# Tensor-product sums by five column-tiled matmuls per edge tile, with the product's scalar part put together by a constant matrix

## The chip, the cores and the metric

The kernel runs on one core of a Trainium2 chip. The time is the device time in microseconds (us) of one execution; the time before is the median of three runs, 1883.51 us (1879.14 to 1885.42). The engines of the core run side by side, each in the order of its own instructions, and meet at semaphores: TensorE (PE for its matmuls, PEld for its weight loads), VectorE (DVE), ScalarE (ACT), GpSimd (POOL) and SyncE (SP), the last two mostly issuing transfers here.

## What is computed

Four graph layers run one after another on 625 nodes and 20,000 edges sorted by receiver, each on a normalised copy of `x` and each added to `x`. The change lies in the third, a tensor product of node features with edge directions:

```python
s0, s1 = x0[sender], x1[sender]            # 128 scalars, 128 vectors of 3 per edge
y0, y1 = edge_attrs[:, 0:1], edge_attrs[:, 1:4]
p1 = w1 * s0 * y0
p2 = (w2 * s0)[:, :, None] * y1[:, None, :]
p3 = w3[:, :, None] * s1 * y0[:, None, :]
p4 = w4 * einsum('eum,em->eu', s1, y1) / SQRT3     # a sum over the vector's 3 parts
msg0 = segment_sum(concatenate([p1, p4], -1), receiver)
msg1 = segment_sum(concatenate([p2, p3], 1), receiver)
o0, o1 = _lin_irreps(msg0, msg1, W_out0, W_out1)
```

`w1` to `w4` come from a small network on eight radial features of each edge (`mlp` in the kernel). So for each receiver eight rows of 128 numbers are summed: one for p1, three for p2, three for p3, and one for p4, which is itself a sum of three products.

## The kernel before

The edges stand in 160 tiles of 125 (`NT`), four tiles to a group (`G`, 40 groups), eight to a step of the gathers and masks. Because the edges are sorted by receiver, the receivers of a group lie within a window of `W` = 32 nodes, which begins at `base_of(g)`. The third layer is `layer2_near`, and its main loop goes over pairs of tiles (80 of them):

- `rows` (line 230 issues it) gathers the senders' rows of the next eight tiles, by GpSimd's indirect transfers.
- `hots` makes the masks on VectorE: `eq` has a 1 where an edge's receiver is the window's node (line 819), and `ohy` holds four masks, `eq` times each of the edge's four attributes y0, y1x, y1y, y1z (line 826).
- `product` makes for each tile the weights `tpw` by a matmul of 64 rows (line 834), the two tiles of a pair on the two halves of the array, and from it on VectorE `msg` of eight blocks: `m[:, 0, 0:4]` is w1 s0 and the three w3 s1, `m[:, 1, 0:4]` is w2 s0 and the three w4 s1 (in two operations, lines 839 and 841).
- `scatter2`, two pairs behind, multiplies the masks with these blocks and sums over the edges of the tile (line 856). A mask has 32 columns, so the result fills 32 rows of a bank: four such column groups of the array, each with its own 32 output rows, hold different sums (`tile_position`). The accumulator `sum` is of 128 rows by three blocks of 128 columns; a group of four tiles is summed in it.
- `evict` copies it by ScalarE (line 873), and `collect`, another two pairs behind, turns it by TensorE (line 881) and adds it to the window's columns of `mT2` on VectorE (line 884).
- `radial` (lines 786 and 791) runs the small network for later tiles, in between.
- `nodes` does the last part for 125 nodes as soon as their last group is collected: output matmuls from `mT2` (line 912; `order` tells which two of its eight rows belong together), the norm, transposes (line 925), and two tables for the next layer (line 932).

Before, `scatter2` issues eight matmuls per tile, and the scalar part p4 is summed over its three products in the accumulator itself, since the three go to the same place. In row r of the column groups and block c, `add(r, c, q, v)` sums mask q times `v`:

| column group | block 0 | block 1 | block 2 |
|---|---|---|---|
| 0 | p1 | p3 x | p3 y |
| 1 | p3 z | p2 x | |
| 2 | p2 y | p2 z | |
| 3 | p4 (three matmuls) | | |

The instructions of each engine are put in order when the program is built, by a scheduler that follows data and buffers; in this layer no order is held by hand. Buffers: two `sum` banks, two shared by `mlp` and `trs`, four of `tpw`; seven `msg` tiles.

Of the kernel before, what the change touches and what calls it, by code (L numbers as in the profile page):

```python
# [9 lines left out]
F32 = mybir.dt.float32  # L10
# [17 lines left out]
MUL = 128  # L28
# [115 lines left out]
def gnn_body(ctx: ExitStack, tc: tile.TileContext, a: dict, out: bass.AP, consts, near: bool):  # L144

    nc = tc.nc
# [603 lines left out]
    def layer2_near(w2s, w1ab, wm3a, uh, h, tab, loads):  # L750

        W = 32
        NS = NT // (2 * G)
        with tc.tile_pool(name="layer2n", bufs=2) as lp, \
                tc.tile_pool(name="ps2n", bufs=1, space=bass.MemoryType.PSUM) as pp:
            def ps2(name):
                return pp.tile([128, 512], F32, tag="ps", name=name, bufs=2)
# [41 lines left out]
            got, sums, ohs, msgs = {}, {}, {}, {}  # L799

            def base_of(g):
                return min(max(math.ceil(g * G * PACE - SLACK), 0), N - W)
# [41 lines left out]

            def scatter2(s, i):

                g = 2 * s + i // 2
                if i % 2 == 0:
                    sums[g] = pp.tile([128, 3 * MUL], F32, tag="sum", name="sum", bufs=2)
                A = sums[g]  # L850
                for j in (2 * i, 2 * i + 1):
                    m, oh = msgs.pop((s, j)), ohs[s][0]
                    done = set()

                    def add(r, c, q, v):
                        nc.tensor.matmul(A[r * W:(r + 1) * W, c * MUL:c * MUL + v.shape[1]], oh[:, j, q, :], v,  # L856
                                         start=j % G == 0 and r not in done, stop=j % G == G - 1,
                                         skip_group_check=True, tile_position=(0, r * W))
                        done.add(r)

                    add(0, 0, 0, m[:, 0, 0:3, :].rearrange("p k u -> p (k u)"))
                    add(1, 0, 0, m[:, 0, 3, :])
                    add(2, 0, 2, m[:, 1, 0, :])
                    add(3, 0, 1, m[:, 1, 1, :])
                    add(1, 1, 1, m[:, 1, 0, :])
                    add(2, 1, 3, m[:, 1, 0, :])
                    add(3, 0, 2, m[:, 1, 2, :])
                    add(3, 0, 3, m[:, 1, 3, :])

            def evict(g):  # L870
                v = lp.tile([128, 3 * MUL], F32, tag="sv", name="sv")
                for n, c in ((128, 0), (96, 1), (32, 2)):
                    nc.scalar.copy(v[:n, c * MUL:(c + 1) * MUL], sums[g][:n, c * MUL:(c + 1) * MUL])
                sums[g] = v

            def collect(g):
                v = sums.pop(g)
                t = ps2("trs")
                o = 0
                for n, c in ((128, 0), (96, 1), (32, 2)):  # L880
                    nc.tensor.transpose(t[:, o:o + n], v[:n, c * MUL:(c + 1) * MUL], ident[:n, :n])
                    o += n
                b = base_of(g)
                nc.vector.tensor_add(mT[:, :, b:b + W], t[:, :o].rearrange("p (k n) -> p k n", n=W),
                                     mT[:, :, b:b + W])
# [2 lines left out]

            last_of = [max(g for g in range(NG) if base_of(g) < (c + 1) * P) for c in range(NC)]
            so = 1.0 / (math.sqrt(2.0 * MUL) * 10.0)  # L890
            order = ((0, 3), (5, 4), (2, 7), (6, 1))
            h3 = node.tile([P, NC, D], F32, tag="h", name="h3")
            tabs = [dram.tile([N, D], F32, tag=v, name=v) for v in ("xs", "xd")]
            stats = {}
# [50 lines left out]
            for i in range(len(pairs) + LAG + 2):  # L945
                if i < len(pairs):
                    s, j = pairs[i]
                    product(s, j)
                    q, step = divmod(i, 2 * G)
                    if 2 <= 2 * q < NS - 2 and step in (1, 3, 5):  # L950
                        radial(q + 1, step // 2)
                    if s + 1 < NS:
                        if j == 0:
                            rows(s + 1)
                        hots(s + 1, j)
                if 0 <= i - LAG < len(pairs):
                    s, j = pairs[i - LAG]
                    scatter2(s, j)
                    if j % 2:
                        evict(2 * s + j // 2)  # L960
                if 0 <= i - LAG - 2 < len(pairs):
                    s, j = pairs[i - LAG - 2]
                    if j % 2:
                        collect(2 * s + j // 2)
                for c in range(NC - 1):
                    step = i - (2 * last_of[c] + LAG + 3)
                    if 0 <= step < 5:
                        nodes(c, step)
                if i in loads:
                    loads[i]()  # L970
# [462 lines left out]
    with tc.tile_pool(name="wts3", bufs=1) as wts:  # L1433
# [3 lines left out]
        if near:  # L1437
# [18 lines left out]
            def load_own():  # L1456
                keep(nc.scalar.dma_start(wm3a, chunks(a["L3_gnn_W3"][:D, :])))

            h_tabs = layer2_near(w2s, w1ab, wm3a, uh, h2, tab2, {6: load_nodes, 30: load_edges, 50: load_own})
            layer3_near(wts, wm2, (b1, b2, w1c), h_tabs, uh)  # L1460
        else:
# [44 lines left out]
```

## Time and profile before

| what | value |
|---|---|
| median of the runs | 1883.51 us |
| the profiled execution | 1883.0 us |
| its span | 1881.2 us |
| mean granted TensorE clock | 0.983 |
| third layer's sums (line 856), first and last start | 670.2 and 998.5 us |
| busy from 660 to 1000 us: TensorE matmuls / VectorE / ScalarE / GpSimd | 321 / 245 / 71 / 197 of 340 us |
| line 856, recorded passes (two for each matmul) | 2560 |
| line 881, the three turns of each group | 120 |
| line 884, the addition | 40 of 421 ns |

The profile is of one execution. A group of instructions is named by line, engine, operation and tiles (`sum<-msg,ohy` writes `sum` from `msg` and `ohy`), a shape is partitions by columns, and "x32" counts instructions. A matmul of 32-bit numbers is recorded as two passes, each with its own weight load (LDWEIGHTS); a transpose is one. The ends of matmuls are modelled, so the spacing of starts tells more than the lengths. In the chain of work that ended last, each instruction is followed back to what released it; "issue" is time in which an engine waited for nothing that the profile shows. The idle time ahead of an instruction is put down to its releaser.

### The profile page before, as it was taken

The page shows a single profiled execution, that of the slowest core. Times are in us where ns is not written, and L with a number is a line of the kernel's source. Part 1 is how long each engine was busy: PE and PEld are TensorE (multiplying, and loading weights), DVE is VectorE, ACT ScalarE, POOL GpSimd, SP SyncE. Part 2 cuts the span into 40 slices and gives each one's busy share as a digit, 9 for nine tenths or more (in the row PEclk, how much of TensorE's full clock was granted, in tenths as well). Part 3 has the DMA queues.
Part 4 walks back from the last instruction along what each step waited for, and adds up shares of the span by engine and source line. Part 5 has one row for each costly group of instructions (what it writes and reads, how often), then busy time and mean ns, then how long its engine had stood idle before and what let it go on. Part 6 is the DMA issues. An engine that isn't in the chain of part 4 may idle for free.

```text
span 1881.2 us, 25801 instructions
## 1 busy us (share of the span) xinstructions
PE 1772.1 (94%) x10688; PEld 960.7 (51%) x10688; DVE 1074.1 (57%) x1877; ACT 741.3 (39%) x856; POOL 809.9 (43%) x478
## 2 busy tenths in 40 slices
PE   5999999999999999999999989999999999999993
PEld 5999844444444444445455444444454444545441
DVE  8999611001100267768774657786676676666655
ACT  1122211000000312222221766767776777668670
POOL 0000000000000077556543688888887888788200
PEclk9999999999999989999999989999999999999996
DMA  2000103003000176565443589666675666666200
GB/s 70 2 2 2 52 0 140 0 0 93 2 0 0 30 187 162 139 146 161 125 119 98 116 150 172 127 122 119 109 132 114 115 132 116 109 119 125 36 0 13
DMA packets 157223, 162.68 MB, mean 86 GB/s; under 512 B 97546, under 2 KB 104059, under 8 KB 157096
## 3 DMA queue, kind: packets, MB, share of 16 engines
q0 software_dynamic: 131584, 119.48, 32.4%
q1 hardware_dynamic: 20100, 32.69, 5.7%
q10 hardware_dynamic: 5412, 8.77, 1.7%
q8 instruction: 86, 1.41, 0.3%
q14 instruction: 41, 0.34, 0.1%
HBM read 155.11 MB, written 5.12 MB: 85 GB/s over the span
## 4 chain that ended last, share of the span: by engine, by line
PE 83%; DVE 11%; ACT 2%; DMA 2%; issue 1%; POOL 0%; DVEq 0%; SPq 0%; ACTq 0%; POOLq 0%
PE z L1243 29%; PE agg L557 9%; PE hb L544 7%; PE sum L856 7%; PE tpw L834 5%; DVE rh L441 4%; PE z L1224 4%; PE z L1229 4%; DVE ohs L450 2%; PE agg L1267 2%; PE xsd L932 2%; PE mlp L786 2%; PE agg L533 2%; PE l L509 2%; PE nsum L502 1%
## 5 line engine op out<-in xcount | busy, mean ns | idle before, releaser
L1243 PE MATMUL z<-wm,z 128*125 128x512 f32 x1280 | 556.9, 593 | 2.7 <-DVE z L1362 2.7
L1243 PEld LDWEIGHTS z<-wm,z 128*125 128x125 f32 x1280 | 237.5, 188 | 293.5 <-issue 268.8
L230 POOL DMA_INDIRECT g_s<-xs,src_i x160 | 303.4, 1896 | 126.1 <-issue 75.5
L230 POOL DMA_INDIRECT g_s<-xd,dst_i x144 | 300.6, 2087 | 43.9 <-issue 42.0
L798 POOL MEMSET mT<- 128x5000 f32 x1 | 4.3, 4267 | 633.4 <-PE agg L557 633.4
L230 POOL DMA_INDIRECT gup<-up,src_i x160 | 198.1, 1238 | 132.0 <-DVE msg L841 60.6
L455 PE MATMUL q<-rh,ohs 125*128 125x160 bf16 (+1 forms) x2400 | 184.5, 238 | 13.5 <-ACT cnt L467 11.0
L455 PEld LDWEIGHTS <-ohs 125*128 125x128 bf16 x2400 | 180.0, 99 | 17.8 <-issue 15.0
L1245 DVE TENSOR_TENSOR mess<-z,b 125x512 f32<-125x512 f32 x160 | 106.4, 687 | 136.4 <-PE z L1243 136.4
L557 PE MATMUL agg<-hb,adj 125*125 125x512 f32 x400 | 173.6, 592 | 0.0
L547 DVE COPY hb<-hb 125x512 f32<-125x512 f32 x20 | 13.8, 692 | 261.0 <-PE hb L544 261.0
L856 PE MATMUL sum<-msg,ohy 125*32 125x128 f32 (+1 forms) x2560 | 146.0, 303 | 8.5 <-issue 6.9
L841 DVE TENSOR_TENSOR msg<-tpw,gup 125x768 f32<-125x768 f32 x160 | 152.0, 950 | 0.0
L856 PEld LDWEIGHTS sum<-msg,ohy 125*32 125x32 f32 x2560 | 101.2, 109 | 86.7 <-issue 85.7
L1231 DVE TENSOR_SCALAR z<-z,b 128x500 f32<-128x500 f32 (+1 forms) x164 | 108.4, 719 | 59.4 <-PE z L1229 57.5
L544 PE MATMUL hb<-basis,hT 128*125 128x512 f32 x320 | 138.6, 592 | 0.0
L1191 ACT ACTIVATE uz<-uz 128x2000 f32<-128x2000 f32 (+1 forms) x41 | 75.0, 1830 | 153.0 <-DVE uz L1183 153.0
L557 PEld LDWEIGHTS agg<-hb,adj 125*125 125x125 f32 x400 | 74.8, 188 | 94.7 <-issue 94.7
L549 ACT COPY hb<-hb 125x512 f32<-125x512 f32 x20 | 11.7, 586 | 258.3 <-PE hb L544 238.4
L839 DVE TENSOR_TENSOR msg<-tpw,gup 125x256 f32<-125x256 f32 x160 | 67.0, 419 | 62.9 <-PE tpw L834 31.1
L1191 ACT ACTIVATE um<-um 125x2048 f32<-125x2048 f32 x39 | 74.6, 1912 | 71.1 <-DVE um L1183 71.1
L544 PEld LDWEIGHTS hb<-basis,hT 128*125 128x125 f32 x320 | 60.1, 188 | 77.3 <-issue 76.8
(187 smaller groups left out, 2240.5 us busy)
## 6 DMA issues: line engine op xcount, KB each, us to landing
rt<-in_edge_attr SPq DMA_DIRECT2D x76, 125.0 KB
basis<-in_L_gnn_basis SPq DMA_DIRECT2D x8, 1024.0 KB
gup<-up,src_i POOLq DMA_INDIRECT x160
g_s<-xs,src_i POOLq DMA_INDIRECT x160
g_s<-xd,dst_i POOLq DMA_INDIRECT x144
w<-in_L_gnn_W SPq DMA_DIRECT2D x2, 1024.0 KB
loop<-in_L_gnn_loop SPq DMA_DIRECT2D x2, 1024.0 KB
w1ab<-in_L_gnn_W ACTq DMA_DIRECT2D x1, 2048.0 KB
```

What stands on the lines that cost most here:

```text
L230: return nc.gpsimd.indirect_dma_start(out=dst, out_offset=None, in_=table, in_offset=bass.IndirectOffsetOnAxis(ap=idx[:, t:t + 1], axis=0) ...
L441: keep(nc.vector.tensor_mul(rh, eq[:, :, None, :].to_broadcast([P, G, 3 * NQ + 1, W]), parts[:, t0:t0 + G, :, None] .to_broadcast([P, G, 3 ...
L455: nc.tensor.matmul(q[c][:, :n, o:o + W], os_[:, c, :], rh[:, j, q0:q0 + n, :], start=i + j + k == 0, stop=i == 1 and j == G - 1 and k == 2 ...
L544: nc.tensor.matmul(p[:P, :], hT[:, k, s * P:(s + 1) * P], basis[b][:, k, :], start=k == 0, stop=k == KD - 1)
L557: nc.tensor.matmul(acc[c], adj[:, s - 1, l * NB + b, c * P:(c + 1) * P], hb[:, b, :], start=False, stop=s == NC and b == NB - 1)
L834: nc.tensor.matmul(p[:P, :], hid[s // 2][s % 2][rws, i * P:(i + 1) * P], w4[rws].rearrange("p k u -> p (k u)"), start=True, stop=True)
L841: nc.vector.tensor_mul(m[:, :, 1:, :], pv[:, 2:4, None, :].to_broadcast([P, 2, 3, MUL]), g[:, None, 1:, :].to_broadcast([P, 2, 3, MUL]))
L856: nc.tensor.matmul(A[r * W:(r + 1) * W, c * MUL:c * MUL + v.shape[1]], oh[:, j, q, :], v, start=j % G == 0 and r not in done, stop=j % G = ...
L1191: keep(nc.scalar.activation(u, u, AF.Exp))
L1231: keep(nc.vector.tensor_scalar(zv[:, n, f, :], pf[f][:, :ne], b1[:, f:f + 1], None, op0=ALU.add))
L1243: nc.tensor.matmul(p[:P, :], z[:, j // w, f, j % w * P:(j % w + 1) * P], wm2[:, f, :], start=f == 0, stop=f == KD - 1)
L1245: keep(nc.vector.tensor_add(m[:, j, :], p[:P, :], bc["b2"]))
```

## The change

The three products of p4 are no longer added in one place. In the new layout each of the column groups 1 to 3 takes one direction, and one matmul of two blocks sums a p2 and a p4 part with the same mask:

| column group | block 0 | block 1 | block 2 |
|---|---|---|---|
| 0 | p1 | p3 x | p3 y |
| 1 | p2 x | p4, part x | p3 z |
| 2 | p2 y | p4, part y | |
| 3 | p2 z | p4, part z | |

```diff
-                    add(0, 0, 0, m[:, 0, 0:3, :].rearrange("p k u -> p (k u)"))
-                    add(1, 0, 0, m[:, 0, 3, :])
-                    add(2, 0, 2, m[:, 1, 0, :])
-                    add(3, 0, 1, m[:, 1, 1, :])
-                    add(1, 1, 1, m[:, 1, 0, :])
-                    add(2, 1, 3, m[:, 1, 0, :])
-                    add(3, 0, 2, m[:, 1, 2, :])
-                    add(3, 0, 3, m[:, 1, 3, :])
+                    add(0, slice(0, 3), 0, m[:, 0, 0:3, :])
+                    for r in range(1, 4):
+                        add(r, slice(0, 2), r, m[:, 1, 0:r + 1:r, :])
+                    add(1, slice(2, 3), 0, m[:, 0, 3:4, :])
```

So a tile has one matmul of 384 columns, three of 256 and one of 128, where it had one of 384 and seven of 128; the columns in all are the same 1280. The parts of p4 are added when the accumulator is turned: block 1 is not transposed but multiplied by a constant matrix `fold` of 64 columns, the first 32 of which pick column group 0, the last 32 the sum of groups 1 to 3. It is made once, by three small VectorE operations from the identity.

```diff
             def evict(g):
-                v = lp.tile([128, 3 * MUL], F32, tag="sv", name="sv")
-                for n, c in ((128, 0), (96, 1), (32, 2)):
-                    nc.scalar.copy(v[:n, c * MUL:(c + 1) * MUL], sums[g][:n, c * MUL:(c + 1) * MUL])
+                v = lp.tile([128, 3, MUL], F32, tag="sv", name="sv")
+                nc.scalar.copy(v[:, :2, :], sums[g][:, :2, :])
+                nc.scalar.copy(v[:2 * W, 2, :], sums[g][:2 * W, 2, :])
...
+            fold = lp.tile([128, 2, W], F32, name="fold", bufs=1)
+            nc.vector.tensor_copy(fold[:, 0, :], ident[:, :W])
+            nc.vector.tensor_add(fold[:, 1, :], ident[:, W:2 * W], ident[:, 2 * W:3 * W])
+            nc.vector.tensor_add(fold[:, 1, :], fold[:, 1, :], ident[:, 3 * W:])
...
-                o = 0
-                for n, c in ((128, 0), (96, 1), (32, 2)):
-                    nc.tensor.transpose(t[:, o:o + n], v[:n, c * MUL:(c + 1) * MUL], ident[:n, :n])
-                    o += n
+                o = 8 * W
+                nc.tensor.transpose(t[:, :4 * W], v[:, 0, :], ident)
+                nc.tensor.matmul(t[:, 4 * W:6 * W], v[:, 1, :], fold.rearrange("p k n -> p (k n)"), start=True,
+                                 stop=True)
+                nc.tensor.transpose(t[:, 6 * W:o], v[:2 * W, 2, :], ident[:2 * W, :2 * W])
...
-            order = ((0, 3), (5, 4), (2, 7), (6, 1))
+            order = ((0, 5), (1, 4), (2, 6), (3, 7))
```

The turned sums are again eight blocks of 32 columns, in another order, which `order` follows. In the order in which the engines get their instructions, the three `fold` operations stand ahead of the first masks, and three times one matmul of `mlp` stands ahead of line 925 instead of behind line 932; otherwise the sequences are the same but for single exchanges of neighbours on VectorE.

More of the change, by code (lines that the diff above doesn't have):

```diff
@@ L848, in scatter2 @@
                 if i % 2 == 0:
-                    sums[g] = pp.tile([128, 3 * MUL], F32, tag="sum", name="sum", bufs=2)
+                    sums[g] = pp.tile([128, 3, MUL], F32, tag="sum", name="sum", bufs=2)
                 A = sums[g]
@@ L853, in scatter2, with add @@
                     done = set()
-                    def add(r, c, q, v):
-                        nc.tensor.matmul(A[r * W:(r + 1) * W, c * MUL:c * MUL + v.shape[1]], oh[:, j, q, :], v,
+                    def add(r, cs, q, v):
+                        nc.tensor.matmul(A[r * W:(r + 1) * W, cs, :], oh[:, j, q, :], v,
                                          start=j % G == 0 and r not in done, stop=j % G == G - 1,
```

## The prediction, made before the changed kernel ran

> **What bounds the kernel now.** I read the page's busy line and chain first: TensorE is busy 94% of the span and 83% of the chain that ended last, and the tensor product's sums (line 856) are its fourth line. VectorE has 11% of the chain.
>
> ```profile
> PE 1772.1 (94%) x10688; PEld 960.7 (51%) x10688; DVE 1074.1 (57%) x1877; ACT 741.3 (39%) x856; POOL 809.9 (43%) x478
> ...
> PE 83%; DVE 11%; ACT 2%; DMA 2%; issue 1%; POOL 0%; DVEq 0%; SPq 0%; ACTq 0%; POOLq 0%
> ```
>
> The change lies in one stage. Line 856 runs from 670.2 to 998.5 us, so I asked for the chain and the waits from 670 to 1000 us (the chain's shares come out on 340 us).
>
> ```profile
> by line: PE sum L856 41.5%; PE tpw L834 25.9%; PE xsd L932 9.1%; PE mlp L786 7.7%; PE trs L881 6.2%; issue 4.1%; PE o L912 2.4%; PE tr L925 0.9%; DVE ohy L826 0.9%; ACT hT L927 0.7%; DVE mT L884 0.4%; ACT h L201 0.2%; ACT sv L873 0.2%; ACTq
> ```
>
> And of the waits (us in all, times, longest):
>
> ```profile
> DVE msg L839 <- PE tpw L834: 29.2, 19, 2.9
> DVE ohy L826 <- PE sum L856: 18.2, 11, 2.9
> DVE msg L839 <- PE sum L856: 15.7, 8, 2.8
> DVE mT L884 <- PE sum L856: 12.8, 8, 2.6
> PE sum L856 <- issue: 6.9, 24, 0.4
> ```
>
> TensorE's lines are some 94% of the stage. VectorE waits for TensorE; TensorE hardly waits for VectorE. So what TensorE saves on this line is time.
>
> What is it that TensorE spends there? The timeline of TensorE shows a clean burst late in the stage and a torn one early. Columns: start us, us, engine, line, names, shape, count, idle before.
>
> ```profile
> 985.97 1.52 PE L856 MATMUL sum<-msg,ohy 125*32 125x384 f32 x32
> 987.42 1.13 PE L834 MATMUL tpw<-w,hid 64*125 64x512 f32 x4
> 988.48 1.52 PE L856 MATMUL sum<-msg,ohy 125*32 125x384 f32 x32
> 989.92 0.58 PE L881 MATMUL trs<-ident,sv 128*128 128x128 f32 x3
> 990.44 1.13 PE L834 MATMUL tpw<-w,hid 64*125 64x512 f32 x4
> ```
>
> ```profile
> 685.92 0.93 PE L856 MATMUL sum<-msg,ohy 125*32 125x384 f32 x12
> 687.19 1.24 PE L856 MATMUL sum<-msg,ohy 125*32 125x128 f32 x10 [0.34 <-issue]
> 688.67 0.50 PE L856 MATMUL sum<-msg,ohy 125*32 125x128 f32 x7 [0.25 <-issue]
> ```
>
> A burst is two tiles: 16 matmuls, each recorded as two passes (x32), each pass with a weight load. Clean, it takes 987.42 - 985.97 = 1.45 us; the torn one takes 689.87 - 685.92 = 3.95 us, with pauses "issue", that is, nothing that the profile shows. In the single records both loads and matmuls stop for 0.4 to 0.6 us, then some 10 to 13 instructions start within 0.2 us. The windows say where:
>
> ```profile
> 680.00:700.00 20.00, 18.14 (x198) 9.16 (x197) 14.37 (x27) 2.21 (x8) 16.31 (x13) 1.00 0.81 218
> 700.00:720.00 20.00, 18.10 (x180) 8.42 (x180) 12.85 (x23) 3.28 (x10) 13.36 (x12) 1.00 0.94 200
> 860.00:880.00 20.00, 19.33 (x219) 10.08 (x212) 18.23 (x35) 3.33 (x12) 14.06 (x12) 1.00 0.69 188
> 980.00:998.00 18.00, 18.00 (x283) 12.01 (x281) 15.90 (x27) 1.80 (x10) 0.00 (x0) 1.00 0.09 30
> ```
>
> (Busy us and counts of PE, PEld, DVE, ACT, POOL; clock; DMA share; GB/s.) With the gathers over (DMA share 0.09), TensorE starts (283+281)/18 = 31 instructions per us without a pause. From 680 to 720 us, at a DMA share of 0.81 to 0.94, it starts 755/40 = 18.9 per us. The clock is 1.00 in all four. So part of line 856 is not arithmetic; it looks like **instructions arriving too slowly** while the DMA engines are busy.
>
> How much: 41.5% of 340 us is 141 us. The 160 tiles are 80 bursts; clean they take 80 x 1.45 = 116 us. The excess is **25 us**. (Summed over single records, the pauses over 0.2 us inside line 856 make 23 us, in 62 pauses.)
>
> **The change part by part.**
>
> *Five matmuls for eight: arithmetic.* The four 32-column groups of the array work side by side. By shape, a pass over 384 columns takes 493 ns and over 128 columns 276 ns: 217 ns for 256 more columns, 0.85 ns each. Per tile, groups 0 to 3 stream 384, 256, 256, 384 columns before and 384, 384, 256, 256 after. The longest group is the same: 2 tiles x 2 passes x 384 x 0.85 = 1.30 us of the 1.45. Only the last group changes: in single records 128-column passes follow each other at 109 ns in a group and 384-column passes at 323 ns, so group 3 was last with 12 x 109 = 1308 ns; now group 1, with four passes of some 216 (estimate, between those two) and four of 109, is 1300 and starts earlier. I take 0.02 us per burst, 80 x 0.02 = **-1.8 us**.
>
> Here a rule gives another sum. "TensorE: Matmul & The Clock Gate" (The mechanism) says that matmuls start strictly in program order. Then a tile's chain, each start no earlier than the one ahead, would be 323 + 8 x 109 = 1195 ns before and 323 + 3 x 216 + 109 = 1080 after: -0.115 x 160 = -18 us. But it would make the clean burst 2.4 us, and the row has 1.45; groups run ahead of each other here. I keep -1.8.
>
> *Five for eight: instructions.* A burst has 64 recorded instructions before, 40 after. A cycle of two bursts with two products (8 each) and a collect (6, then 8) has 150 before, 104 after; its clean time is 991.50 - 985.97 = 5.53 us by the late starts. That asks for 27 per us before, 19 after. The supply of the worst stretch is 18.9. So before it must stall (150/18.9 = 7.9 us), after hardly (5.5). Bounds: if pauses only go down with the instructions, 24/64 of 25 = 9.4 us; if they go entirely, 25. I take the middle, **-17 us**, because inside a burst it still asks for 40/1.43 = 28 per us.
>
> Against it speaks "Runtime: NRT & Kernel Launch" (Instruction fetch mechanics): each sequencer fetches its next 16 KiB ahead, and fetching is hidden behind dispatch. By that rule the pauses are no supply problem and this part is 0; the whole sum would be +1.5. The rows show pauses that follow instruction density and DMA share, so I go with the rows, and keep 0 as a rival.
>
> *Collect.* Three transposes (0.52 us from start to the next line's start, 989.92 to 990.44) become a transpose, a matmul by the constant matrix in two passes, and a transpose of 64 rows. One more load-and-matmul: the nearest row is line 912's 128-column matmuls, 16 in about 1.98 us, 0.12 each: 40 x 0.12 = +4.8 us, high end. Low end: "TensorEngine Tiling (Array Packing)" (Key Properties) has a change of tiling mode drain the array; before, 32-row weights stand ahead of the 64-row products, now 64 rows ahead of 64 rows, which happens after 25 of 40 collects. If the wait of about 0.12 us between the two goes, 25 x 0.12 = 3.0 comes back, +1.8. I take about the middle, **+3**.
>
> *Eviction.* Three ACT copies become two. ACT is busy 71 of 340 us and collect comes two steps later: 0. With that cover gone a late copy would cost up to 0.3 us x 40.
>
> *Constants.* Three small VectorE operations ahead of the stage, like the 287 ns of line 819: 0 to 0.9 us, taken as **+0.3**.
>
> *Order.* The engines' orders keep their shape; three times one matmul of the radial network moves into TensorE's wait for the normalised rows ahead of line 925: 0. POOL and SP issue the same transfers in the same order.
>
> *What is late next.* In 860 to 880 us VectorE is busy 18.2 of 20. Its cycle, 4 x (0.34 + 0.86) for the products at their start-to-start, 0.33 for the addition, about 0.8 for masks, is 5.9 us against TensorE's 5.5 (6.5 where the radial network runs, 3 in 5). So some of what TensorE gains it will wait for: **+2**.
>
> Sum: -1.8 - 17 + 3 + 0.3 + 2 = **-13.5 us**. The profiled execution took 1883.0 (span 1881.2), the median is 1883.5: **1869.5 us**. What follows layer 2 waits for its last node block, so the gain reaches the end.
>
> **The rivals.**
> A. *Nearly all pauses go* (-25) and VectorE keeps up: -25 - 1.8 + 1.8 + 0.3 = -25, 1858. For it: demand 19 against supply 18.9. Against: VectorE's 91%. It shares the forecast's cause.
> B. *The pauses are not instruction supply* (for instance operands read while transfers write), and stay: -1.8 + 3 + 0.3 = +1.5, 1884.5. For it: the same DMA share, the rule above. Against: the batches of 10 to 13 starts.
> C. *Collect becomes expensive.* If its four load-and-matmul steps (two transposes, two passes by the constant matrix) don't overlap at all, they take their rows' full lengths, 323 + 3 x 247 ns = 1.06 us (128x128 row 323; 96 and 32 columns 249 and 244) instead of 0.52: 40 x 0.54 = +22 us. With the pauses giving only their lower bound, 22 - 1.8 - 9.4 + 0.3 = +11, 1894. It decides once the pauses give less than 20. Against: today's three steps do overlap (0.52 against a sum of 0.82).
> D. The change doing less than said is excluded by the order: 1280 matmuls become 800.
>
> **How the numbers follow.** Forecast 0.54, A 0.18, B 0.16, C 0.12. About 0.3% (5.7 us, 1877.9 to 1889.2) can be told from no change. Faster: forecast and A, less the forecast's weak end (0.04) : 0.68, plus a little of B: 0.70. Same: B and that end, 0.19. Slower: C, 0.11. The range goes from A with a little more, 1856, to B with the dearer collect, 1886; the forecast alone is 1861 to 1877.
>
> **What would show it.** Line 856: 1600 passes, a clean burst of x20 in 1.42 to 1.45 us, its chain share near 36% of a stage 14 us shorter; "issue" ahead of it under 3 us; windows at a DMA share over 0.8 with TensorE starts no longer torn. Collect at 0.55 to 0.63 us. Torn bursts as long as before mean B; collect near 1.06 means C; VectorE as what TensorE waits for means the give-back was too small.

## The result, and the profile after

| | kernel before | changed kernel |
|---|---|---|
| median of the runs | 1887.58 us (10 runs) | 1877.31 us (10 runs) |
| ratio, with its 95% interval | | 0.9942 [0.9926, 0.9958] |
| the profiled execution | 1883.0 us | 1877.4 us |
| its span | 1881.2 us | 1875.6 us |
| third layer's sums, first and last start | 670.2 and 998.5 us | 677.8 and 991.0 us |

The changed kernel is faster by 0.58%, some 10 us by the medians and 5.6 by the two profiled executions. The stage of the sums is shorter by much more, and it begins later. Cut at places that both traces have (us):

| stretch | before | after | difference |
|---|---|---|---|
| start to line 561 of layer 1's last block (same code) | 643.8 | 647.6 | +3.8 |
| from there to the first gather of layer 2 | 14.5 | 19.8 | **+5.3** |
| first gather to last sum | 340.2 | 323.6 | **-16.6** |
| last sum to the end | 882.7 | 884.6 | +1.9 |

The first and last rows are the same instructions in both kernels and differ from run to run by as much in the other traces. Two rows have to be explained.

First the stage. The busy line of the changed kernel (us, share of the span, instructions) and its chain by engine:

```profile
PE 1767.1 (94%) x9768; PEld 945.8 (50%) x9768; DVE 1079.7 (58%) x1880; ACT 740.1 (39%) x816; POOL 811.7 (43%) x478
...
PE 80%; DVE 12%; DMA 3%; ACT 2%; issue 1%; POOL 1%; DVEq 0%; POOLq 0%; another core or an unknown queue 0%; SPq 0%; ACTq 0%
```

TensorE has 920 instructions fewer (10688 to 9768) but only 5 us less to do: the arithmetic is the same. Its share of the chain went from 83% to 80%, and DMA's from 2% to 3%. The chain from 670 to 1000 us by line, then its two longest pieces (start us, us, what):

```profile
by line: PE sum L857 33.1%; PE tpw L834 23.0%; PE xsd L936 9.3%; PE mlp L786 8.5%; DMA gup<-up,src_i 5.9%; PE o L916 3.0%; issue 3.0%; PE trs L883 3.0%; PE trs L886 2.4%; PE trs L884 2.0%; DVE msg L841 1.5%; POOL gup L230 1.0%; PE tr L929 0
...
675.13 5.51 DMA gup<-up,src_i
690.32 14.00 DMA gup<-up,src_i
```

The sums' share fell from 41.5% to 33.1% of 330 us, and a line has come in that the chain of before did not have: 5.9%, 19.5 us, on the arrival of gathered rows. The timeline of TensorE, late in the stage (start us, us, engine, line, names, shape, count):

```profile
975.50 1.50 PE L857 MATMUL sum<-msg,ohy 125*32 125x384 f32 x20
976.92 0.33 PE L883 MATMUL trs<-ident,sv 128*128 128x128 f32 x1
977.09 0.33 PE L884 MATMUL trs<-fold,sv 128*128 128x64 f32 x2
977.35 0.27 PE L886 MATMUL trs<-ident,sv 64*128 64x64 f32 x1
977.36 1.17 PE L834 MATMUL tpw<-w,hid 64*125 64x512 f32 x4
978.46 1.49 PE L857 MATMUL sum<-msg,ohy 125*32 125x384 f32 x20
```

A burst is 20 passes, 1.42 us from start to start (975.50 to 976.92); this collect takes 0.44 us (976.92 to 977.36) where one at the same place took 0.52. And early in the stage, where the bursts of before were torn:

```profile
692.04 1.49 PE L857 MATMUL sum<-msg,ohy 125*32 125x384 f32 x20
693.47 0.33 PE L883 MATMUL trs<-ident,sv 128*128 128x128 f32 x1
693.63 0.33 PE L884 MATMUL trs<-fold,sv 128*128 128x64 f32 x2
693.90 0.27 PE L886 MATMUL trs<-ident,sv 64*128 64x64 f32 x1
694.01 1.80 PE L834 MATMUL tpw<-w,hid 64*125 64x512 f32 x4
695.74 1.49 PE L857 MATMUL sum<-msg,ohy 125*32 125x384 f32 x20
701.63 2.04 PE L834 MATMUL tpw<-w,hid 64*125 64x512 f32 x2 [4.40 <-DVE msg L841]
705.85 2.04 PE L834 MATMUL tpw<-w,hid 64*125 64x512 f32 x2 [2.18 <-DVE msg L841]
```

The bursts are whole (692.04 to 693.47), although the DMA engines are as busy as before. But then TensorE stands still: from the burst at 695.74, over by 697.2, to 701.63, and again up to 705.85. The line says "<-DVE msg", a wait for VectorE, and the list of waits says what VectorE waited for (us in all, times, longest):

```profile
DVE msg L839 <- DMA gup<-up,src_i: 26.0, 7, 16.8
...
PE tpw L834 <- DVE msg L841: 6.6, 2, 4.4
```

So TensorE waited for VectorE, and VectorE for gathered rows that had not landed. The windows show the same (busy us and counts of PE, PEld, DVE, ACT, POOL; clock; DMA share; GB/s):

```profile
680.00:700.00 20.00, 17.23 (x151) 8.93 (x148) 13.51 (x22) 1.58 (x6) 16.04 (x14) 1.00 0.79 220
700.00:720.00 20.00, 16.19 (x94) 6.47 (x95) 14.89 (x27) 2.66 (x6) 14.03 (x12) 0.66 0.99 202
860.00:880.00 20.00, 20.00 (x187) 9.78 (x189) 18.26 (x36) 3.71 (x10) 14.99 (x12) 1.00 0.68 187
970.00:988.00 18.00, 18.00 (x159) 8.86 (x158) 14.97 (x26) 1.64 (x5) 0.88 (x1) 1.00 0.16 51
```

From 700 to 720 us the DMA engines have no room left (0.99), TensorE starts 189 instructions (of a shorter sequence) where before it started 360, and its granted clock is 0.66. In the two later windows it is never idle.

### The profile page after: what moved, and what is told of

The parts are those of the page before. It is cut to its first block, busy times and chain, and to the rows that moved or that the text cites. A ratio compares the mean times of both kernels' runs of the same rounds, so it can differ in the third digit from the quotient of the medians.

```text
span 1875.6 us, 23924 instructions
## 1 busy us (share of the span) xinstructions
PE 1767.1 (94%) x9768; PEld 945.8 (50%) x9768; DVE 1079.7 (58%) x1880; ACT 740.1 (39%) x816; POOL 811.7 (43%) x478
## 4 chain that ended last, share of the span: by engine, by line
PE 80%; DVE 12%; DMA 3%; ACT 2%; issue 1%; POOL 1%; DVEq 0%; POOLq 0%; another core or an unknown queue 0%; SPq 0%; ACTq 0%
PE z L1247 29%; PE agg L557 9%; PE hb L544 7%; PE sum L857 6%; DVE rh L441 4%; PE tpw L834 4%; PE z L1233 4%; PE z L1228 4%; DVE ohs L450 2%; PE agg L1271 2%; PE agg L533 2%; PE l L509 2%; PE xsd L936 2%; PE mlp L786 2%; PE q L455 1%
## 5 line engine op out<-in xcount | busy, mean ns | idle before, releaser
L230 POOL DMA_INDIRECT g_s<-xs,src_i x160 | 297.9, 1862 | 127.7 <-issue 76.0
L230 POOL DMA_INDIRECT g_s<-xd,dst_i x144 | 307.4, 2135 | 43.9 <-issue 42.0
L857 PE MATMUL sum<-msg,ohy 125*32 125x256 f32 (+2 forms) x1600 | 124.5, 389 | 0.0
L857 PEld LDWEIGHTS sum<-msg,ohy 125*32 125x32 f32 x1600 | 74.3, 109 | 84.5 <-issue 59.0
L834 PE MATMUL tpw<-w,hid 64*125 64x512 f32 x320 | 101.0, 656 | 6.7 <-DVE msg L841 6.6
```

The lines of the kernel that those rows point to most:

```text
L230: return nc.gpsimd.indirect_dma_start(out=dst, out_offset=None, in_=table, in_offset=bass.IndirectOffsetOnAxis(ap=idx[:, t:t + 1], axis=0) ...
L834: nc.tensor.matmul(p[:P, :], hid[s // 2][s % 2][rws, i * P:(i + 1) * P], w4[rws].rearrange("p k u -> p (k u)"), start=True, stop=True)
L857: nc.tensor.matmul(A[r * W:(r + 1) * W, cs, :], oh[:, j, q, :], v, start=j % G == 0 and r not in done, stop=j % G == G - 1, skip_group_che ...
```

## Experiments

Every experiment ran beside the kernel before on the same chip, in four groups. The first thing that they showed is that the gain depends on where it is measured. Each group ran on another chip, and each of these chips was met once, so that the chip and the occasion can't be told apart; "chip" stands for both below. The ratio is to the kernel before on that chip:

| kernel | the kernel before there, us | ratio [95%] |
|---|---|---|
| fold_mul | 1853.0 (chip 0) | 0.9999 [0.9987, 1.0011] |
| before_fold | 1853.0 (chip 0) | 1.0035 [1.0022, 1.0047] |
| eight | 1853.0 (chip 0) | 1.0044 [1.0027, 1.0062] |
| both | 1853.0 (chip 0) | 0.9962 [0.9949, 0.9975] |
| before_again | 1853.5 (chip 1) | 1.0004 [0.9990, 1.0018] |
| after_again | 1853.5 (chip 1) | 1.0025 [1.0010, 1.0041] |
| eight_mul | 1853.5 (chip 1) | 1.0001 [0.9990, 1.0011] |
| before_short | 1853.5 (chip 1) | 1.0041 [1.0023, 1.0059] |
| eight_2 | 1880.8 (chip 5) | 1.0029 [1.0017, 1.0042] |
| after_2 | 1853.8 (chip 6) | 1.0025 [1.0008, 1.0041] |
| fold_mul_2 | 1853.8 (chip 6) | 0.9992 [0.9977, 1.0007] |
| both_2 | 1853.8 (chip 6) | 0.9954 [0.9939, 0.9970] |

The unchanged kernel before takes 1853 us on three chips (called fast below), and 1881 to 1888 on chip 5 and in the measurement of the result (called slow). On two of the fast three the changed kernel itself ran, and it is no gain at all: 1.0025, twice. The expectations of the first group (chip 0) were written before this was known.

### The constants

The second row to be explained, +5.3 us ahead of the first gather. The timeline of the changed kernel there:

```profile
647.63 4.26 POOL L798 MEMSET mT<- 128x5000 f32 x1 [637.34 <-PE tr L739]
...
648.16 3.77 DVE L875 COPY fold<-ident 128x32 f32<-128x32 f32 x1
648.25 3.68 DVE L876 TENSOR_TENSOR fold<-ident 128x32 f32<-128x32 f32 x1
648.35 3.58 DVE L191 BATCH_NORM_STATS2 stats<-x 125x6 f32<-125x512 f32 x1
...
651.99 0.19 DVE L877 TENSOR_TENSOR fold<-fold,ident 128x32 f32<-128x32 f32 x1
...
653.34 0.47 PE L739 MATMUL tr<-ident,h 125*128 125x125 f32 x1 [3.57 <-ACT h L747]
```

GpSimd's memset of `mT2` runs from 647.63 to 651.89. The copy that begins `fold` starts beside it and takes 3.77 us for 32 columns, to 651.93; the operation behind it and line 191's statistics of the last node block come out with it, and the third operation follows. TensorE then waits 3.57 us for what hangs on them, where before it waited 0.69 at that line. In before_fold the three operations were put into the kernel before, which has no use for them:

```diff
+            fold = lp.tile([128, 2, W], F32, name="fold", bufs=1)
+            nc.vector.tensor_copy(fold[:, 0, :], ident[:, :W])
+            nc.vector.tensor_add(fold[:, 1, :], ident[:, W:2 * W], ident[:, 2 * W:3 * W])
+            nc.vector.tensor_add(fold[:, 1, :], fold[:, 1, :], ident[:, 3 * W:])
```

> The kernel before with the three constant-matrix operations alone added at the same place; nothing reads the matrix. Theory 1 (the copy is held by GpSimd's memset): the copy takes 3.5 to 4 us, the first gather comes some 5 us later, ratio 1.0027. Theory 2 (only these operations' own length, under 1 us): ratio 1.000.

They alone cost 1.0035, 6.5 us of 1853 (2.2 to 4.7 thousandths, 4 to 9 us). In fold_mul, and again in fold_mul_2, the changed kernel makes its first constant by a multiplication, which gives the same numbers since the identity holds only 0 and 1:

```diff
-            nc.vector.tensor_copy(fold[:, 0, :], ident[:, :W])
+            nc.vector.tensor_mul(fold[:, 0, :], ident[:, :W], ident[:, :W])
```

> The changed kernel with the first of the three constant-matrix operations written as a VectorE multiplication of the identity with itself instead of a copy. In the changed kernel's trace that copy took 3.77 us and ended with GpSimd's memset of mT2 (647.63 + 4.26 us), and the stage's first gather came 19.8 us after the last block's line 561, against 14.6 before. Theory 1 (the copy, and only the copy, is held until GpSimd's memset ends): the three operations take about 0.2 us each, first gather about 14.8 us after that line, and the time falls by about 5 us: ratio to the kernel before 0.9915. Theory 2 (any VectorE operation put ahead of the node block's statistics delays it): the operations still end together with the memset, ratio unchanged at 0.994.

> The changed kernel with its first constant made by a multiplication instead of the copy. The copy is held beside GpSimd's memset and costs 5 to 6 us on any chip, so this stands 0.003 below the changed kernel: 0.990 to 0.993 where the kernel before takes 1880 us or more, 1.000 where it takes 1853. If the copy's cost is hidden where the chip is slower, the two are equal.

The same place in fold_mul's timeline:

```profile
645.41 4.27 POOL L798 MEMSET mT<- 128x5000 f32 x1 [635.12 <-PE tr L739]
...
645.95 0.18 DVE L875 TENSOR_TENSOR fold<-ident 128x32 f32<-128x32 f32 x1
646.05 0.18 DVE L876 TENSOR_TENSOR fold<-ident 128x32 f32<-128x32 f32 x1
646.15 0.69 DVE L191 BATCH_NORM_STATS2 stats<-x 125x6 f32<-125x512 f32 x1
...
646.75 0.17 DVE L877 TENSOR_TENSOR fold<-fold,ident 128x32 f32<-128x32 f32 x1
```

Beside the same memset the multiplication takes 0.18 us, and from line 561 to the first gather it is 14.4 us in both runs (14.5 and 16.3 in the two traces of the kernel before, 19.8 to 21.0 in every kernel with the copy). By the ratios 1.0025 becomes 0.9992 on chip 6: 6 us. So it is the copy. That the memset holds it is read from its end: in each of the six traces that have the copy it ends 0.04 us behind the memset's end. No run moved the memset away. In the Trainium skill, "SBUF — State Buffer" (SBUF: two separate sides) states such a rule: VectorE and GpSimd share a port pair that one of them holds for a whole instruction, and a 32-bit copy within SBUF uses it. The traces agree with it, 3.77 us against 0.18. The step had been weighed without it.

### Five matmuls or eight

In eight each matmul of two blocks is two of one block. Layout, collect and constants stay those of the changed kernel, and a tile has eight matmuls again:

```diff
-                        add(r, slice(0, 2), r, m[:, 1, 0:r + 1:r, :])
+                        add(r, slice(0, 1), r, m[:, 1, 0:1, :])
+                        add(r, slice(1, 2), r, m[:, 1, r:r + 1, :])
```

> The changed kernel with each matmul of 256 columns split into two of 128: eight matmuls per tile again, with the same columns in the same column groups, the same operands and the same eviction and collect. Theory 1 (instruction supply): pauses over 0.2 us inside the sums' line come back to about 20 us (23 before, 3.5 after), bursts are torn again from 680 to 720 us, and the time is about that of the kernel before, plus 5 us for the constants' copy, less 1 us of collect: ratio 1.002. Theory 2 (pauses come from operand reads beside the transfers, or the gain came from the layout): pauses stay near 3.5 us, ratio 0.994 as for the changed kernel.

It takes 1.0044, but the copy is in it, worth some 1.003, so that little is left. To see the matmuls without the copy, eight_mul has the multiplication too, and the two kernels themselves ran on the same chip:

> The changed kernel with the multiplication for the copy and with each matmul of 256 columns split into two of 128, so eight per tile. Theory 1 (without pauses the number of matmuls does not matter, the column groups run side by side): within 0.2% of the changed kernel with the multiplication, ratio to the kernel before 1.000 where there are no pauses; 1.000 to 1.003 where there are. Theory 2 (each matmul has a cost of its own of some 25 ns on the path): 3 x 160 x 2 passes x 0.025 = 24 us, ratio 1.013.

> The kernel before, unchanged, profiled beside the following runs, because the earlier experiments' time of the kernel before (1853.0 us) was 35 us under its time beside the changed kernel (1887.6 us). Theory 1 (the pauses inside the sums' line belong to some sessions of the chip and not to the kernel alone): where the time is about 1853 us, pauses over 0.2 us inside the line sum to under 5 us, against 23 us in the first trace. Theory 2 (the pauses are a property of the kernel and the 35 us come from elsewhere): they sum to about 20 us again.

> The changed kernel, unchanged, beside the kernel before. Theory 1 (its gain was the pauses, and the constants' copy costs 5 to 6 us): where the kernel before has no pauses to lose it is slower by the copy, ratio 1.003; where it has 20 us of them, 0.994. Theory 2 (its gain is in the arithmetic or the collect): ratio 0.994 in either case.

eight_mul is at 1.0001 on chip 1, as fold_mul with its five matmuls is at 0.9999 on chip 0. On these chips five or eight makes no difference that is clear of the noise, and the reason is in the windows of before_again, which is the kernel before:

```profile
680.00:700.00 20.00, 19.59 (x268) 11.73 (x265) 16.85 (x31) 3.35 (x14) 16.03 (x14) 1.00 0.87 229
700.00:720.00 20.00, 16.34 (x163) 8.43 (x163) 15.72 (x29) 2.71 (x7) 13.06 (x12) 0.83 0.94 191
```

From 680 to 700 us TensorE starts 268 + 265 = 533 instructions, 26.7 per us, at a DMA share of 0.87; in the first profile of the same kernel it was 395 at 0.81. Its timeline there has no torn burst:

```profile
685.50 1.52 PE L856 MATMUL sum<-msg,ohy 125*32 125x384 f32 x32
686.95 0.59 PE L881 MATMUL trs<-ident,sv 128*128 128x128 f32 x3
...
688.52 1.52 PE L856 MATMUL sum<-msg,ohy 125*32 125x384 f32 x32
689.97 1.13 PE L834 MATMUL tpw<-w,hid 64*125 64x512 f32 x4
```

There was nothing to save. What was needed was a chip that has the pauses, and eight_2, the kernel eight once more, came to one:

> The changed kernel with each matmul of 256 columns split into two of 128 once more, to meet a session in which the kernel before takes some 1885 us and not 1853. Where it takes 1885: theory 1 (instruction supply) has about 20 us of pauses inside the sums and a ratio near 1.002; theory 2 (the gain of the changed kernel there came from elsewhere) has pauses near 3 us and 0.994. Where it takes 1853 both have hardly a pause and 1.003 to 1.005, as before.

Its ratio there is 1.0029 to the kernel before, and in the timeline of TensorE bursts are torn again, at the same "issue":

```profile
729.76 1.00 PE L857 MATMUL sum<-msg,ohy 125*32 125x384 f32 x16
731.02 1.17 PE L857 MATMUL sum<-msg,ohy 125*32 125x384 f32 x11 [0.26 <-issue]
732.50 0.49 PE L857 MATMUL sum<-msg,ohy 125*32 125x128 f32 x5 [0.31 <-issue]
```

The 32 passes from 729.76 take over 3.1 us. The measure of the pauses that is comparable across all traces is the time between consecutive TensorE starts within the sums, added up over the single records from the first gather to the last sum (us):

| kernel, and where | matmuls per tile | time within the sums | first gather to last sum |
|---|---|---|---|
| before, first profile | 8 | 131.1 | 340.2 |
| eight_2, chip 5 | 8 | 118.0 | 331.9 |
| after, the profile of the result | 5 | 100.8 | 323.6 |
| before_again, chip 1 | 8 | 102.2 | 307.3 |
| eight, chip 0 | 8 | 102.0 | 308.2 |
| after_again, chip 1 | 5 | 100.9 | 309.4 |
| after_2, chip 6 | 5 | 100.9 | 308.1 |
| fold_mul_2, chip 6 | 5 | 100.9 | 308.6 |
| both_2, chip 6 | 5 | 99.7 | 300.0 |

Between consecutive sums, eight matmuls lose 16 us (118.0 - 102.0) to 29 us (131.1 - 102.2) where the program is slow and nothing where it is fast; five lose nothing in either. eight_2 has the new layout, the new collect, the copy and the same columns, so what decides is how many matmuls the columns are cut into. The ratios say the same: 1.0029 and 0.9942, each against the kernel before beside it, are 16 us apart, and 118.0 and 100.8 are 17. Two reservations stay. The changed kernel itself wasn't met on chip 5, and the chip of the result isn't known; that it is a slow one is read from the kernel before, which took 1887.6 us beside it. And each matmul brings its own weight loads, so that fewer instructions to issue and fewer loads to read can't be told apart here.

The traces do speak on one explanation, that the instructions are fetched too slowly. They record the fetches; of the lists of transfer queues (packets, MB, share of 16 engines), the line before and the line after:

```profile
q8 instruction: 86, 1.41, 0.3%
```

```profile
q8 instruction: 79, 1.29, 0.3%
```

The packets are of 16 KB, and 86 and 79 of them stand against 21,376 and 19,536 matmuls and loads, some 250 to a packet in both, so by its count this queue is TensorE's. In the first trace of the kernel before, 63 pauses of over 0.2 us lie inside the sums, in which neither a matmul nor a load starts, and 26 packets fall into the same stretch, of 1.2 us each as against 1.1 in before_again. Only 8 of the 63 pauses come within 0.3 us of a packet, no more than chance would give (about 11), and from 674.7 to 691.2 us, around the torn burst at 685.92, there is none. A shortage of fetched instructions is not what the pauses look like. Nor are the transfers slower: the 4 KB packets of the gathers' queue take 0.24 us in the mean in both traces.

after_2 ran the changed kernel once more:

> The changed kernel again, beside the kernel before on the same chip. The gain comes from pauses inside the sums' line, which only some chips show. If the kernel before takes 1880 us or more here, some 20 us of pauses are there to be saved and the constants' copy costs 6: ratio 0.993 to 0.996. If the kernel before takes 1853 us, there are no pauses to save and the copy's cost is all that is left: 1.0025. A theory in which the change saves by its arithmetic or layout expects the same ratio on both.

The chip was a fast one and the ratio 1.0025, as its second case said. A theory in which the change saves its 10 us by its arithmetic or its layout is ruled out by this run together with the first result.

### Fewer bytes to gather: inconclusive

If the pauses come with busy DMA engines, taking the bytes away should take the pauses away. before_short is the kernel before in which, after the first twelve tiles, a gather fetches 64 of 512 columns into one of twelve fixed buffers; the rest of the buffer is old, so the layer's values differ.

```diff
-                    got[s].append(lp.tile([P, D], F32, tag="gup", name="gup", bufs=12))
-                    gather(tab, src_i, s * 2 * G + j, got[s][-1])
+                    t = s * 2 * G + j
+                    got[s].append(ring[t % 12])
+                    w = D if t < 12 else 64
+                    gather(tab.rearrange("n (a u) -> (n a) u", u=w), src_i, t, ring[t % 12][:, :w])
```

> The kernel before with the senders' gathers, after the first twelve, fetching 64 of 512 columns into twelve fixed buffers: the number of gathers is the same, but most rows of the product are old ones, so the layer's values differ. Theory 1 (pauses need busy DMA engines): with the DMA share well under 0.3 from 700 to 980 us there is no pause inside the sums beyond 2 us in all, in any session, and no wait for a gather beside the load of w1ab. Theory 2 (the pauses come from instruction density alone): they are as large as in the unchanged kernel of the same session.

The DMA share fell to 0.27 to 0.42, and the time within the sums is 103.2 us: no pauses. But the chip was one without pauses in the first place, and the fixed buffers delayed the early gathers (TensorE stood still for 10.4 us up to 690.3); 1.0041 says nothing of either theory. What a pause has to do with the transfers stays open.

### The gathers' wait

The chain of the changed kernel waits 14 us for gathered rows from 690.32 on. At 688.6 us, with pair 6 of the loop, one transfer of 2 MB for the next layer (`w1ab`) is issued from ScalarE's queue. both is fold_mul with that transfer in eight pieces of 256 KB, one every second pair:

```diff
-            def load_nodes():
-                keep(nc.scalar.dma_start(w1ab, chunks(a["L3_gnn_W1"][:2 * D, :])))
+            def load_nodes(k):
+                keep(nc.scalar.dma_start(w1ab[:, k, :], a["L3_gnn_W1"][k * 128:(k + 1) * 128, :]))
...
-            h_tabs = layer2_near(w2s, w1ab, wm3a, uh, h2, tab2, {6: load_nodes, 30: load_edges, 50: load_own})
+            h_tabs = layer2_near(w2s, w1ab, wm3a, uh, h2, tab2, 
+                                      {30: load_edges, 50: load_own,
+                                       **{6 + 2 * k: (lambda k=k: load_nodes(k)) for k in range(2 * KD)}})
```

> The changed kernel with the multiplication for the copy, and the 2 MB load of w1ab, issued in one transfer at pair 6, issued in eight of 256 KB at pairs 6, 8, ... 20. In the changed kernel's trace TensorE waits from 690 to 704 us for a gather that shares the DMA engines with this load. Theory 1 (the load delays the gathers and the delay is now in the open): that wait falls from 14 to under 4 us and the time by some 8 us more than without the copy: ratio 0.987. Theory 2 (the gathers are limited by GpSimd's issue, 1.52 us for each, so the load is hidden anyway): ratio as with the multiplication alone, 0.9915.

> Multiplication in place of the copy, and the 2 MB of weights fetched in eight pieces. The gathers wait less: another 0.003 to 0.004 below, so 0.986 to 0.989 where the kernel before takes 1880 us or more, 0.996 where it takes 1853. If the gathers' wait in the open is bound by the transfers in all and not by their bunching, it equals the kernel with the multiplication alone.

It is the fastest version: 0.9962 and 0.9954. Against fold_mul on the same chips that is 0.37% and 0.38%, 7 us; as the two differ in this transfer alone, its bunching is shown to be the cause. Windows of fold_mul_2 and of both_2, same chip:

```profile
680.00:700.00 20.00, 15.46 (x123) 6.92 (x119) 12.32 (x23) 1.81 (x6) 14.01 (x12) 0.82 0.99 238
```

```profile
680.00:700.00 20.00, 19.73 (x176) 9.44 (x176) 18.52 (x34) 2.64 (x8) 16.17 (x13) 1.00 0.80 203
```

With one transfer TensorE is busy 15.5 of 20 us, DMA at 0.99 and the clock at 0.82; with pieces 19.7 us at 0.80 and 1.00. The chain of both_2 has no piece of gathered rows left:

```profile
by line: PE sum L857 35.6%; PE tpw L834 25.2%; PE xsd L936 11.1%; PE mlp L786 8.1%; PE uh L906 4.2%; PE trs L883 3.0%; PE o L916 3.0%; PE trs L886 2.5%; PE trs L884 2.1%; issue 1.1%; PE tr L929 0.9%; DVE z L1235 0.5%; ACT L1195 0.4%; ACT L1
```

The kernel before has this wait on a fast chip, too (four pieces, 21.2 us of before_again's chain); in its first profile it has none. That TensorE was late itself there is one reading of this, but eight_2, with pauses as well, has a wait of 15.4 us, so it isn't settled. both was not met on a slow chip, so what it brings there wasn't measured.

## Why the prediction came out as it did

It said 1869.5 us and a gain of 13.5; measured were 1877.3, and a gain of 10.3 by the medians on a base 4 us higher. The likeliest case was the one that happened, but the parts of the sum are off in ways that partly cancel, and that the number came so near is in part luck.

- **Arithmetic, -1.8:** right. The clean burst is 1.42 us where it was 1.45, and on chips without pauses the sums take 100.9 for 102.2 us. The rule of strict program order, which would have given -18, is refuted by the same two figures.
- **Pauses, -17, bounds 9.4 to 25:** that pauses go with the number of matmuls is borne out by eight_2 against the changed kernel; that the instructions come too slowly is not, as far as it means their fetching. The rule set against it, that fetching is hidden, isn't contradicted by the packets; the conclusion drawn from it, no gain, is. The size was low: time within the sums fell by 30.3 us, of which some 1.5 are arithmetic, beyond both bounds, since inside the sums five matmuls have no pauses at all. The bounds rested on a slip, too: the chain's shares are of the window, 330 us, so 41.5% is 137 us and not 141, and the excess by that sum 21 and not 25. "The supply of the worst stretch is 18.9" is wrong as a figure of the chip: on chip 1 the same instructions came at 26.7 per us at a DMA share of 0.87. Rival B, that the pauses stay, is ruled out for the measured run; yet on both chips of the experiments where the changed kernel ran, its forecast of no gain is what happened, for another reason: there are no pauses.
- **Collect, +3:** both halves of the estimate are in the traces, and they nearly cancel. Ahead of a burst, 9 of the 40, a collect takes 0.63 us for 0.52, and ahead of the tables and the output matmuls, five more, it is dearer by as much: the 0.12 of one more step. Ahead of products, 25 of them, it takes 0.44 for 0.52, so there 0.19 are saved against the 0.12 estimated, while what follows the products comes 0.05 later. In all that is some +1 us. Rival C falls.
- **Eviction, 0:** nothing in the waits speaks against it.
- **Constants, +0.3, bounds 0 to 0.9:** this term failed. "Three small VectorE operations ahead of the stage, like the 287 ns of line 819" took a row with two inputs for a copy. That row ran beside the same memset (at 644.38 us in the first trace, for 0.28) in its plain length, so it could not show what a copy meets there. It cost 5 to 7 us.
- **What is late next, +2:** something was, but not VectorE's own work. Between the first two traces some 11 us of TensorE's gain came back as waits ahead of products (7.5 between products, 3.8 between a burst and a product), 6.6 of them in the two waits shown above, behind gathered rows and the 2 MB transfer. "VectorE waits for TensorE; TensorE hardly waits for VectorE" was a reading of that one trace. Rival A, nearly all pauses gone and VectorE keeping up, had the first half right and was stopped here.

So by the traces the sums gave -30.3, the rest of the stage took 13.7 back (forecast: -18.8 and +5), and the constants ahead of it took 5.3 (forecast: +0.3): -11.3 in all for -13.5. Of the signs named beforehand, whole bursts, the x20 in 1.42 us and the missing "issue" ahead of the sums came true; the share of 36% was 33.1%, and a collect of 0.55 to 0.63 us came in 9 of 40. The luck is also in the place: on a fast chip the same prediction would have missed.

Three things stay open. What a pause is isn't shown, nor why only some chips have them. And the changed kernel, whole bursts and all, still takes 15 us longer in the stage on the slow side (323.6 against 308.1): 6.1 of these are ahead of the output matmuls, 5.8 ahead of products, 3.6 ahead of the tables' matmuls and 2.2 ahead of collects. Of the matmuls' waits ahead of the output the profile puts 3.4 us down to VectorE's addition and 2.9 to "issue" again, so outside the sums pauses remain.

## What to carry to other kernels

A pause that the profile can't name may belong to the place of measurement and not to the program alone: before a gain is built on it, run the unchanged kernel on a second chip, and expect the gain only where the pauses are. Fewer and wider matmuls cost nothing measurable here where there were no pauses, and where there were, they took them away inside the sums. And no small operation is free by its size: price it by a row of the same operation, and look at what the engine that shares its port does in that microsecond.

## What the runs showed of the hardware

- A VectorE copy of 32 columns took 3.77 us, to 0.04 us behind the end of a GpSimd memset of 4.26 us, in six traces of six; a multiplication of the same columns at the same place took 0.18.
- The same program took 1853 us on three chips and 1881 on a fourth, and the profiles put the difference into one stage: first gather to last sum, 307 to 312 against 332 to 340 us with eight matmuls per tile (before_short aside), while from the last sum to the end it is 880 to 885 us in every trace.
- A stop of TensorE has a price after it: in 700 to 720 us the changed kernel's clock was granted at 0.66, and one tile's product took 1.96 us to the next line's start (705.85 to 707.81) where two tiles' together take 1.10 at full clock (977.36 to 978.46). In the eleven traces in which TensorE stood idle for over 1 us at a time between 680 and 740 us, its clock was once halved there, for 3 to 17 us; in the three without such a stop (the first one of the kernel before, both, both_2) it was not.
- A collect of three transposes (128, 96 and 32 rows) took 0.52 us to the next line's start; one of four steps that ends in 64 rows took 0.44 ahead of products of 64 rows, and 0.63 ahead of a burst.
